# Two changes around a 1x1 convolution: seven block products in place of eight, and a residual added by accumulating transfers

## The chip, the cores and the metric

The kernel runs on one core of one Trainium2 chip. The core has five engines that each work through their own instructions in order: TensorE (matrix products; in the profile PE, its weight loads PEld), VectorE (DVE), ScalarE (ACT), GpSimd (POOL) and SyncE (SP), which here only issues transfers. POOL issues transfers too, on a queue of its own. Engines wait for each other and for transfers on semaphores. The metric is the device time of one execution in microseconds; given is the median of the runs. All data are 32-bit floats.

## The reference

Two layers on `x` of shape (4, 1024, 32, 32), that is 4 batches of N = 1024 tokens with C = 1024 channels. The first layer is attention with normed and rotated queries and keys, the second three convolutions with batch norms:

```python
# layer 0
q, k, v = split(x @ w_qkv.T + b_qkv)
q, k = rmsnorm(rope(q)), rmsnorm(rope(k))
ctx = softmax(q k^T / 8) v            # 16 heads of 64
out = rmsnorm(ctx @ w_proj.T) * norm_out_w
x1  = out + x                         # residual of layer 0
# layer 1
h = relu(bn(conv1x1(x1, w1) + b1))    # 1024 -> 256 channels
h = relu(bn(conv3x3(h, w2) + b2))
h = bn(conv1x1(h, w3) + b3)           # 256 -> 1024
y = relu(x1 + softplus(residual_scale) * h)
```

The batch norms take mean and variance over all four batches, so no value of the first 1x1 convolution can be used before the last batch's is there.

## The kernel before

All activations lie channels by tokens: a batch is eight rows of tiles [128 channels, 1024 tokens]. `half[0]` and `half[1]` are its two halves of 512 tokens, `NH` = 4 is half of the eight rows. The batches go one after the other through the projections of q, k and v, attention and the output projection `y`. The large projections (`project2`) are products of 2x2 blocks done with seven products in place of eight, in two levels; sums of blocks of the activations are made by VectorE, sums of weight blocks lie ready in DRAM. The first convolution (L850, `conv1`) is done plainly.

For batches 0 to 2, y after its norm is stored to DRAM (`x1d`), and `x` is added to it there by accumulating transfers that POOL issues during the next batch's attention (`add_residual`, L1034). Batch 3 has no attention after it. Its norm (`last_norm`, L826 to L841) works on y in place: `inverse_rms` makes the sum of squares over channels by a TensorE product with ones (`ss_y`, L666), then root, reciprocal and a round through DRAM back into `total` (tile `sqy`); then for each half and row VectorE multiplies y by it (L834) and adds `x` (L835) from the tile `xr`, which SP has loaded (L1095), and SP stores the result to `x1d` (L836). y of batch 3 stays in SBUF and is the input of its own convolution.

While that norm runs, TensorE does the first convolution of batches 1, 2 and 0, whose inputs are read back from `x1d` by `read_back` (tile `x` for batch 1, `back` for 2, `x_back` for 0), then that of batch 3. A call of `conv1` makes one of 2 x 2 output tiles of a batch (128 of 256 channels by 512 tokens) with eight matmuls into one bank of the pool `o2`; ScalarE takes it out with the bias, VectorE makes its statistics (L859) and SP stores it to `h1d` (L860). For batches 0 and 1 the tiles come back as `h1l` (L1128) and are filled into padded tiles for the 3x3 convolution (L1131, L1142, L1202). The weights `w_c_last` are four chunks of the ring `w` of eight; the weights `w3` of the last convolution (L1309) come into the same ring.

The order of the work is written out by hand: TensorE, POOL and, through this part, VectorE and ScalarE keep the order in which the program issues instructions. `after(n, step)` runs a step n products later, `waiting` holds steps that are taken one by one as there is room (`pace`), and `product_done` moves this clock. Only SP's transfers are ordered by a scheduler, at build time; on the chip SP then works through them strictly in that order, and each waits for what it needs. A transfer issued by SP also waits for the one eight places before it. Short-lived tiles of 128x512 come from the pool `tmp` with four buffers: a new one waits until the earliest free buffer's last reader, often a store, is done.

Of the kernel before, what the change touches and what calls it, by code (L numbers as in the profile page):

```python
# [12 lines left out]
AF = mybir.ActivationFunctionType  # L13
ALU = mybir.AluOpType
# [4 lines left out]
P = 128  # L19
B, C, H, W = 4, 1024, 32, 32  # L20
N = H * W
NT = C // P
HD = 64
NHP = C // (2 * HD)
CH = 512
NCH = N // CH
# [3 lines left out]
NPT = PL // P  # L30
# [31 lines left out]
NH = NT // 2  # L62
NG = NT // 2
QH = P // 4
SUMS = ("S2", "S1", "S3", "S4")
# [20 lines left out]
def program(ctx, tc, x, wblk, w2, w3, vecs, cos, sin, out, bad):  # L86


    nc = tc.nc
# [6 lines left out]
    x1d = dram.tile([NT, P, B * N], F32, name=f"x1d{u}")  # L96
    h1d = dram.tile([NPT, P, B * N], F32, name=f"h1d{u}")
# [13 lines left out]
    def col(name, i=0):  # L111
        return vec[:, COL[name] + i : COL[name] + i + 1]
# [30 lines left out]
    h1stats = const.tile([P, NPT, B * NCH, nc.vector.BN_STATS_DIM], F32, name="h1stats")  # L143
# [9 lines left out]
    with tc.tile_pool(name=f"st{u}", bufs=2) as st, ExitStack() as s:  # L153
# [25 lines left out]
        yt = {}  # L179
        half = [slice(c * CH, (c + 1) * CH) for c in range(NCH)]  # L180
# [17 lines left out]
        def bank(kind, name):  # L198
            pool, shape = psum[kind]
            return pool.tile(shape, F32, tag=kind, name=name)  # L200

        def temp(name):
            return tmp.tile([P, CH], F32, tag="tmp", name=name)

        def big_temp(name):
            return big.tile([P, N], F32, tag="big", name=name)

        def load_x(b, c, rows=range(NT)):
            for i in rows:
                nc.sync.dma_start(xs[b][:, i, half[c]], x[b, i * P : (i + 1) * P, half[c]])  # L210

        def chunk(name):
            return wring.tile([P, NH, P], F32, tag="w", name=name)
# [28 lines left out]
        TT = 0.21  # L242
        later, waiting = [], deque()
# [5 lines left out]
        def after(n, step):  # L249
            later.append((pace["at"] + n, step))  # L250

        def product_done(share=1.0):
            pace["at"] += share
            pace["room"] = min(pace["room"] + share, 1.2)
            due = [s for at, s in later if at <= pace["at"]]
            later[:] = [(at, s) for at, s in later if at > pace["at"]]
            for step in due:
                step()
            while waiting and pace["room"] > 0 and not pace["hold"]:
                next_waiting()  # L260

        def next_waiting():
            cost, step = waiting.popleft()
            spend(cost)
            step()
# [5 lines left out]
        def sums(ts, bs, i):  # L271

            at, low = slice(i, i + 2), slice(i + NH, i + NH + 2)
            b11, b12, b21, b22 = (bs[:, r, h] for r in (at, low) for h in half)
            t1, t2, t4 = (t[:, at, :] for t in ts)
            nc.vector.tensor_tensor(t1, b12, b11, ALU.subtract)
            nc.vector.tensor_tensor(t2, b22, t1, ALU.subtract)
            nc.vector.tensor_tensor(b12, b22, b12, ALU.subtract)
            nc.vector.tensor_tensor(t4, b21, t2, ALU.subtract)
# [377 lines left out]
        def inverse_rms(total, eps, scale, name, then):  # L657


            r = temp(f"rms_{name}")[:, :QT]  # L660
            row = inv_d[norms_done.pop(0)]

            def root():
                o = bank("o2" if name in ("q_0", "k_0") else "o1", f"ss_{name}")[:, :QT]
                for q in range(4):
                    nc.tensor.matmul(  # L666
                        o[q * QH : (q + 1) * QH, :], ones[:, :QH], total[:, q * QT : (q + 1) * QT],
                        start=True, stop=True,
                    )
                nc.scalar.activation(r, o, AF.Sqrt, bias=eps, scale=scale)  # L670
                after(0.5, invert)

            def invert():
                spend(3 * TT)
                nc.vector.reciprocal(r, r)
                nc.gpsimd.dma_start(row.rearrange("(q t) -> q t", q=4), r[::QH, :])
                nc.gpsimd.dma_start(total, row.partition_broadcast(P))
                after(2.5, then)

            after(4, root)  # L680
# [145 lines left out]

            inverse_rms(total, eps_rms, 1.0 / C, f"y_{b}", then)

        def last_norm(b, total, ys, xr):


            def norm(f, at):
                y = ys[:, f, at]
                nc.vector.scalar_tensor_tensor(y, y, col("ow", f), total[:, at], ALU.mult, ALU.mult)  # L834
                nc.vector.tensor_tensor(y, y, xr[:, f, at], ALU.add)  # L835
                nc.sync.dma_start(x1d[f, :, b * N + at.start : b * N + at.stop], y)  # L836

            def then():
                waiting.extend([(2 * TT, lambda f=f, at=at: norm(f, at)) for at in half for f in range(NT)])

            inverse_rms(total, eps_rms, 1.0 / C, f"y_{b}", then)  # L841

# [3 lines left out]
        def conv1(b, f, c, w, ys, then=None):  # L846
            o = bank("o2", f"c1_{b}_{c}_{f}")
            for i in range(NT):
                ih, ii = divmod(i, NH)
                nc.tensor.matmul(  # L850
                    o, w[f][ih][:, ii, :], ys[:, i, half[c]], start=(i == 0), stop=(i == NT - 1)
                )
                if i == NH - 1:
                    product_done()
            h = temp(f"h1_{b}_{c}_{f}")
            nc.scalar.activation(h, o, AF.Identity, bias=col("b1", f))

            def stats():
                nc.vector.bn_stats(h1stats[:, f, b * NCH + c, :], h)  # L859
                nc.sync.dma_start(h1d[f, :, b * N + c * CH : b * N + (c + 1) * CH], h)  # L860
                if then is not None:
                    then()

            after(1, stats)
            product_done()

        def norm_of(stats, g, be, name):
# [48 lines left out]
        def read_back(b, rows=range(NT)):  # L916
            for i in rows:
                nc.sync.dma_start(back[b][:, i, :], x1d[i, :, b * N : (b + 1) * N])

        def x_tile(b):  # L920
            return xp.tile([P, NT, N], F32, tag="x", name=f"x_{b}")

        def t_tiles(b):
            return [tp.tile([P, NH, CH], F32, tag=f"T{i}", name=f"t{i}_{b}") for i in range(3)]

        def v_room(name):
            return kv.tile([P, N // P, C], F32, tag="v", name=name)
# [47 lines left out]
        room = v_room("rq_0")  # L975
        for b in range(B):
# [67 lines left out]
            room = v_room(f"to_{b}")  # L1044
# [12 lines left out]
            if b + 1 < B:  # L1057
                xs[b + 1] = x_tile(b + 1)
                ts[b + 1] = t_tiles(b + 1)
                rows = (0, 1, 4, 5, 2, 3, 6, 7)  # L1060
                for j in range(NT):

                    def load(b=b, i=rows[j]):
                        for c in range(NCH):
                            load_x(b + 1, c, (i,))

                    after(3 + 1.5 * j, load)
                for i in range(0, NH, 2):

                    def queue(b=b, i=i):  # L1070
                        waiting.append((7 * TT, lambda: sums(ts[b + 1], xs[b + 1], i)))

                    after(3 + 1.5 * (2 * i + 3) + 2, queue)
            else:
                back = {1: x_tile(b + 1)}
                for i in range(NT):
                    after(8 + 1.5 * i, lambda i=i: read_back(1, (i,)))
            if b == 0:
                weight_parts([parts_of[WK][1]], 2, 0, 4, pieces_of(room[:, 3 * NT // 4 :, :]))
            yt[b] = kp.tile([P, NT, N], F32, tag="k", name=f"y_{b}")  # L1080
# [3 lines left out]
            ty = qk_proj(b, WP, q_all, tc_, None, yt[b], "y", None, two)  # L1084
            if b + 1 < B:
                o_norm(b, ty, yt[b])
            else:
                xr = v_room("xr")
                last_norm(b, ty, yt[b], xr)

        back[2] = kv.tile([P, NT, N], F32, tag="q", name="back")
        read_back(2)
        w = conv1_weights("last")
        for i in range(NT):
            nc.sync.dma_start(xr[:, i, :], x[B - 1, i * P : (i + 1) * P, :])  # L1095
        for b in (1, 2, 0):
            if b == 0:
                back[0] = x_tile("back")
                read_back(0)
            for c in range(NCH):  # L1100
                for f in range(NPT):
                    conv1(b, f, c, w, back[b])
        rest()
        if bad is not None:
            dt = temp("dens")
# [169 lines left out]
        for b in range(B):  # L1275
            steps = []
            if b + 1 < B:
                steps = transform(b + 1, 0) + transform(b + 1, 1)
# [5 lines left out]
            for f in range(NPT):  # L1284
                for h in range(2):
# [14 lines left out]
                    steps = steps[4:]  # L1300
# [9 lines left out]
            if b == 0 and bad is not None:  # L1310
                o = ps.tile([P, CH], F32, tag="mm", name="fit")
# [20 lines left out]
        for f in range(NT):  # L1332
            if f > 0 and f + 2 < NT:
                load_x1(f + 2)
            stats = st.tile([P, B * NCH, nc.vector.BN_STATS_DIM], F32, tag="s3", name=f"s3_{f}")
# [5 lines left out]
            for i, k in order:  # L1341
                b, c = divmod(i, NCH)
                nc.tensor.matmul(  # L1343
                    os[i], w3t[k][f // NH][:, f % NH, :], h2[b, k][:, half[c]],
                    start=(k == 0), stop=(k == NPT - 1),
# [3 lines left out]
                h = h3s[f % 2][:, b, half[c]]  # L1349
# [89 lines left out]
```

## Time and profile before

| | |
|---|---|
| median of 3 runs (2713.77 to 2715.1) | 2714.19 us |
| the profiled execution | 2712.96 us |
| its span, first to last instruction | 2711.0 us |
| TensorE busy | 2665.8 us, 98% of the span |
| VectorE busy | 2171.9 us, 80% |
| ScalarE / POOL busy | 1096.3 us, 40% / 448.5 us, 17% |
| mean granted TensorE clock | 0.996 |

The busy shares are means over stages. By stage around the change (from a table of windows, us from the span's start; busy is us of the stage's length):

| stage | length | PE | DVE | ACT | DMA share, GB/s |
|---|---|---|---|---|---|
| convolution of batch 1, 2359.78 to 2387.60 | 27.82 | 27.82 | 8.77 | 5.90 | 0.96, 362 |
| of batch 2, to 2415.10 | 27.50 | 27.50 | 24.12 | 2.75 | 0.90, 305 |
| of batch 0, to 2442.60 | 27.50 | 27.50 | 2.78 | 2.75 | 0.22, 80 |
| of batch 3, to 2470.10 | 27.50 | 27.50 | 12.59 | 5.42 | 0.48, 144 |

TensorE is busy without a break; VectorE is so only while batch 2 is done, when it norms y of batch 3; the DMA engines are full through the first two stages.

### The profile page before, as it was taken

Reading aid. Unit: us, or ns where it says so; the run is one execution under the profiler, and the core shown is the slowest. Engines: PE = TensorE matmul, PEld = TensorE weight load, DVE = VectorE, ACT = ScalarE, POOL = GpSimd, SP = SyncE. Lnnn points to the kernel's source line nnn. Section 1 sums busy time; section 2 is a strip of 40 time slices with the busy share of each in tenths; the row PEclk is TensorE's granted clock in tenths of the full one; section 3 lists DMA queues with packets and bytes.
Section 4 is the critical chain, followed back from the end, with each engine's and each line's share of the span. In section 5 each row is a group of like instructions: output and inputs, shape, how many; then the busy total and the mean of one; then the engine's idle time right before and its main releaser. Section 6 shows DMA issues by size and latency. Waiting matters only on the chain. (4 is left out here: it accounts for less than half of the span.)

```text
span 2711.0 us, 32574 instructions
## 1 busy us (share of the span) xinstructions
PE 2665.8 (98%) x11410; PEld 1658.3 (61%) x11410; DVE 2171.9 (80%) x2516; ACT 1096.3 (40%) x1520; POOL 448.5 (17%) x552
## 2 busy tenths in 40 slices
PE   9999999899999999999999999999999999999997
PEld 4448533387888433588886333888884335846843
DVE  5578899988798877888878877877888878646987
ACT  2222555323352555333343555233525653312266
POOL 2562223302111211100111211100111211000000
PEclk9999999999999999999999999999999999999999
DMA  7897645577677341456765420666783314662165
GB/s 277 315 308 223 182 151 170 181 242 257 220 206 212 67 93 32 143 152 221 188 184 153 84 58 17 212 200 177 188 233 82 71 40 130 195 242 86 63 226 210
DMA packets 245965, 453.54 MB, mean 167 GB/s; under 512 B 28385, under 2 KB 117265, under 8 KB 245793
## 3 DMA queue, kind: packets, MB, share of 16 engines
q1 hardware_dynamic: 203568, 310.72, 36.6%
q0 software_dynamic: 42224, 140.63, 19.7%
q8 instruction: 94, 1.54, 0.2%
q14 instruction: 79, 0.64, 0.1%
HBM read 316.71 MB, written 96.78 MB: 153 GB/s over the span
## 5 line engine op out<-in xcount | busy, mean ns | idle before, releaser
L768 DVE TENSOR_TENSOR den<-den,p 128x1024 f32<-128x1024 f32 x384 | 470.5, 1225 | 40.7 <-DVE den L766 0.5
L764 ACT ACTIVATE p<-sc 128x1024 f32<-128x1024 f32 x512 | 476.2, 1043 | 53.7 <-PE sc L757 53.6
L757 PE MATMUL sc<-q,k 64*128 64x512 f32 x2048 | 457.5, 596 | 0.0
L757 PEld LDWEIGHTS sc<-q,k 64*128 64x128 f32 x2048 | 190.2, 186 | 265.1 <-issue 121.4
L774 PE MATMUL cx<-p,to 128*64 128x512 f32 x1536 | 340.2, 595 | 0.0
L774 PEld LDWEIGHTS cx<-p,to 128*64 128x64 f32 x1536 | 106.0, 137 | 228.2 <-issue 228.2
L458 PE MATMUL p_y<-q,w_y 128*128 128x256 f32 x928 | 211.9, 382 | 5.6 <-DMA w_y<-in_wblk_dram 4.8
L738 POOL TENSOR_SCALAR q<-q,vec 128x512 f32<-128x512 f32 x64 | 122.7, 1923 | 564.2 <-DVE q L737 564.1
L453 PE MATMUL p_v<-w_v,x 128*128 128x256 f32 x928 | 209.7, 379 | 1.0 <-DVE x L424 1.0
L458 PEld LDWEIGHTS p_y<-q,w_y 128*128 128x128 f32 x928 | 176.9, 191 | 33.7 <-issue 9.7
L453 PEld LDWEIGHTS p_v<-w_v,x 128*128 128x128 f32 x928 | 176.2, 190 | 25.8 <-DVE x L424 1.4
L779 ACT COPY q<-cx 128x512 f32<-128x512 f32 x64 | 37.5, 587 | 357.0 <-PE cx L774 357.0
L458 PE MATMUL p_k<-to,w_k 128*128 128x256 f32 x672 | 153.1, 381 | 3.7 <-ACT to L547 3.7
L458 PE MATMUL p_q<-to,w_q 128*128 128x256 f32 x672 | 152.6, 380 | 0.4 <-ACT q L547 0.3
L458 PEld LDWEIGHTS p_k<-to,w_k 128*128 128x128 f32 x672 | 126.7, 190 | 25.0 <-ACT to L547 6.1
L458 PEld LDWEIGHTS p_q<-to,w_q 128*128 128x128 f32 x672 | 127.1, 190 | 20.3 <-ACT q L512 1.3
L766 DVE TENSOR_TENSOR den<-p 128x1024 f32<-128x1024 f32 x64 | 76.5, 1195 | 77.7 <-ACT p L764 77.7
L805 DVE RECIPROCAL rec<-dn 128x512 f32<-128x512 f32 x32 | 107.3, 3352 | 20.6 <-PE dn L799 20.6
L774 PE MATMUL cx<-p,rq 128*64 128x512 f32 x512 | 113.4, 595 | 0.0
L1343 PE MATMUL c<-h,w 128*128 128x512 f32 x256 | 110.3, 592 | 0.9 <-ACT h L1245 0.9
L700 POOL DMA_DIRECT2D k<-ks x64 | 55.4, 1012 | 278.4 <-ACT p L764 96.0
L458 PE MATMUL p_y<-to,w_y 128*128 128x256 f32 x384 | 90.1, 379 | 0.0
(438 smaller groups left out, 4182.2 us busy)
## 6 DMA issues: line engine op xcount, KB each, us to landing
w_v<-wd2f SPq DMA_DIRECT2D x112, 256.0 KB
w_y<-wd2f SPq DMA_DIRECT2D x112, 256.0 KB
w_q<-wd2f SPq DMA_DIRECT2D x84, 256.0 KB
w_k<-wd2f SPq DMA_DIRECT2D x84, 256.0 KB
x<-in_x_dram SPq DMA_DIRECT2D x64, 256.0 KB
q<-qs POOLq DMA_DIRECT2D x64, 256.0 KB, 5.6
k<-ks POOLq DMA_DIRECT2D x64, 256.0 KB, 4.5
inv<-rec SPq DMA_DIRECT2D x256, 64.0 KB
```

The costliest lines, as they stand in the source:

```text
L453: nc.tensor.matmul(o[:, q].rearrange("p (g f) -> p g f", g=2), r[:, i, q * P : (q + 1) * P], wt[:, :, i, :], skip_group_check=True, **at,)
L458: nc.tensor.matmul(o[:, q], wt[:, q, i, :], r[:, i, :], skip_group_check=True, **at)
L700: nc.gpsimd.dma_start(dst[i::2, f, :], other[1 - i :: 2, :], accum_op=ALU.add)
L738: nc.gpsimd.tensor_scalar(cx, cx, col("bv", hp), None, ALU.add)
L757: nc.tensor.matmul(sc[:, j], k_all[d, hp, t * P : (t + 1) * P], q_all[d, hp, at], start=True, stop=bad is not None,)
L764: nc.scalar.activation(p, sc, AF.Exp)
L766: nc.vector.tensor_tensor(d_, probs[0], p, ALU.add)
L768: nc.vector.tensor_tensor(d_, d_, p, ALU.add)
L774: nc.tensor.matmul(o[j * HD : (j + 1) * HD, :], v[:, t, h0 : h0 + HD], probs[t][:, j], start=(t == 0), stop=(t == N // P - 1),)
L779: nc.scalar.copy(q_all[:, hp, at], o)
L805: nc.vector.reciprocal(r, dn)
L1343: nc.tensor.matmul(os[i], w3t[k][f // NH][:, f % NH, :], h2[b, k][:, half[c]], start=(k == 0), stop=(k == NPT - 1),)
```

## The change

*Seven products.* For batches 1, 2 and 0 the 2x2 blocks of the weights (output channels by input rows; `A11` to `A22`) and of the input (`b11`, `b12` the upper rows' halves, `b21`, `b22` the lower ones') are combined into seven products of four matmuls each in place of eight: A11·b11, A12·b21, S2·T2, S1·T1, S4·b22, S3·(b22-b12), A22·(b21-T2). `conv1_sums` makes S1 to S4 from the weights on VectorE once, into the other four chunks of the ring. `t_sums` makes four differences per batch in eight VectorE operations of 128x1024; for batch 1 six of the eight are put into the last output projection, through `waiting`, with T1 in the unused last quarter of that batch's room. The products of a batch go into two banks that keep adding up (`o` of the pool `o1`, `o2`); ScalarE copies intermediate states out between products (`c11`, `c12`, `c22`, `c21`, and `c1p` from the second bank), and VectorE adds the parts. `conv1_rest` is a generator: after its first two products, A11 and A12 of the next batch are put in, then its last three (S4, S3, A22). Batch 0, the last, has none put in between. Batch 0 is read back into the tile `v` in place of the tile `x`.

*Last residual.* `last_norm` works on whole rows of 1024: L834 multiplies, then POOL issues a transfer that adds `x` from DRAM to y in SBUF, and SP's store to `x1d` follows it. `xr` and its loads are gone.

*What the build makes of SP's order.* From the weights of the first convolution on: `back` of batch 2 (8), store of c11 of batch 1, `back` of batch 0 (8), stores of c11 of batch 2, c12, c21 and c22 of batch 1, stores of y rows 1 to 5 (L836), store of c11 of batch 0, stores of y rows 6 to 8, stores of c12, c21 and c22 of batch 2, three w3 loads, store of c12 of batch 0, and then the first `h1l` load. The buffers of `tmp`: ScalarE's c1p of batch 0 takes over the buffer of c12 of batch 2, c21 of batch 2 that of c11 of batch 0.

```diff
@@ -826,17 +826,17 @@
 
             inverse_rms(total, eps_rms, 1.0 / C, f"y_{b}", then)
 
-        def last_norm(b, total, ys, xr):
-
-
-            def norm(f, at):
-                y = ys[:, f, at]
-                nc.vector.scalar_tensor_tensor(y, y, col("ow", f), total[:, at], ALU.mult, ALU.mult)
-                nc.vector.tensor_tensor(y, y, xr[:, f, at], ALU.add)
-                nc.sync.dma_start(x1d[f, :, b * N + at.start : b * N + at.stop], y)
+        def last_norm(b, total, ys):
+
+
+            def norm(f):
+                y = ys[:, f, :]
+                nc.vector.scalar_tensor_tensor(y, y, col("ow", f), total, ALU.mult, ALU.mult)
+                nc.gpsimd.dma_start(y, x[b, f * P : (f + 1) * P, :], accum_op=ALU.add)
+                nc.sync.dma_start(x1d[f, :, b * N : (b + 1) * N], y)
 
             def then():
-                waiting.extend([(2 * TT, lambda f=f, at=at: norm(f, at)) for at in half for f in range(NT)])
+                waiting.extend([(2 * TT, lambda f=f: norm(f)) for f in range(NT)])
 
             inverse_rms(total, eps_rms, 1.0 / C, f"y_{b}", then)
 
@@ -855,13 +855,99 @@
             h = temp(f"h1_{b}_{c}_{f}")
             nc.scalar.activation(h, o, AF.Identity, bias=col("b1", f))
 
-            def stats():
-                nc.vector.bn_stats(h1stats[:, f, b * NCH + c, :], h)
-                nc.sync.dma_start(h1d[f, :, b * N + c * CH : b * N + (c + 1) * CH], h)
+            def done():
+                keep_h1(b, f, c, h)
                 if then is not None:
                     then()
 
-            after(1, stats)
+            after(1, done)
+            product_done()
+
+        def keep_h1(b, f, c, h):
+            nc.vector.bn_stats(h1stats[:, f, b * NCH + c, :], h)
+            nc.sync.dma_start(h1d[f, :, b * N + c * CH : b * N + (c + 1) * CH], h)
+
+        def conv1_sums(w):
+
+            (a11, a12), (a21, a22) = w
+            s2, s1, s3, s4 = (chunk(f"c1_{o}") for o in SUMS)
+            nc.vector.tensor_tensor(s1, a21, a22, ALU.add)
+            nc.vector.tensor_tensor(s2, s1, a11, ALU.subtract)
+            nc.vector.tensor_tensor(s3, a11, a21, ALU.subtract)
+            nc.vector.tensor_tensor(s4, a12, s2, ALU.subtract)
+            return s2, s1, s3, s4
+
+        def t_sums(ys, t1, t2, i, steps=range(4)):
+
+            at, low = slice(i, i + 2), slice(i + NH, i + NH + 2)
+            b11, b12, b21, b22 = (ys[:, r, h] for r in (at, low) for h in half)
+            for out, p, q in [(t1, b12, b11), (t2, b22, t1), (b12, b22, b12), (b21, b21, t2)][steps[0] : steps[-1] + 1]:
+                nc.vector.tensor_tensor(out, p, q, ALU.subtract)
+
+        mine = {}
+
+        def four(o, wt, rows, first, last):
+            for i in range(NH):
+                nc.tensor.matmul(
+                    o, wt[:, i, :], rows(i), start=first and i == 0, stop=last and i == NH - 1,
+                    skip_group_check=True,
+                )
+
+        def conv1_first(b, ys, w):
+
+            o = mine[b] = bank("o1", f"c1_{b}")
+            four(o, w[0][0], lambda i: ys[:, i, half[0]], True, False)
+            h = temp(f"c11_{b}")
+            nc.scalar.copy(h, o)
+            product_done()
+            o2 = bank("o2", f"c1a_{b}")
+            four(o2, w[0][1], lambda i: ys[:, i + NH, half[0]], True, True)
+
+            def done():
+                nc.vector.scalar_tensor_tensor(h, o2, col("b1", 0), h, ALU.add, ALU.add)
+                keep_h1(b, 0, 0, h)
+
+            after(1, done)
+            product_done()
+
+        def conv1_rest(b, ys, w, ss, t1, t2):
+
+            o = mine[b]
+            four(o, ss[0], t2, False, False)
+            h12 = temp(f"c12_{b}")
+            nc.scalar.copy(h12, o)
+            product_done()
+            yield
+            o2 = bank("o2", f"c1s_{b}")
+            four(o2, ss[1], t1, True, False)
+            p5 = temp(f"c1p_{b}")
+            nc.scalar.activation(p5, o2, AF.Identity, bias=col("b1", 1))
+            product_done()
+            yield
+            four(o2, ss[3], lambda i: ys[:, i + NH, half[1]], False, True)
+
+            def done12():
+                nc.vector.scalar_tensor_tensor(h12, o2, col("b1", 0), h12, ALU.add, ALU.add)
+                keep_h1(b, 0, 1, h12)
+
+            after(1, done12)
+            product_done()
+            yield
+            four(o, ss[2], lambda i: ys[:, i, half[1]], False, False)
+            h22 = temp(f"c22_{b}")
+            nc.scalar.copy(h22, o)
+
+            def done22():
+                nc.vector.tensor_tensor(h22, h22, p5, ALU.add)
+                keep_h1(b, 1, 1, h22)
+
+            after(1, done22)
+            product_done()
+            yield
+            four(o, w[1][1], lambda i: ys[:, i + NH, half[0]], False, True)
+            h21 = temp(f"c21_{b}")
+            nc.scalar.activation(h21, o, AF.Identity, bias=col("b1", 1))
+            after(1, lambda: keep_h1(b, 1, 0, h21))
             product_done()
 
         def norm_of(stats, g, be, name):
@@ -1072,9 +1158,19 @@
 
                     after(3 + 1.5 * (2 * i + 3) + 2, queue)
             else:
+
                 back = {1: x_tile(b + 1)}
-                for i in range(NT):
-                    after(8 + 1.5 * i, lambda i=i: read_back(1, (i,)))
+                for j, i in enumerate((0, 1, 4, 5, 2, 3, 6, 7)):
+                    after(3 + 1.5 * j, lambda i=i: read_back(1, (i,)))
+                t1 = room[:, 3 * NT // 4 :, :].rearrange("p a (c t) -> p (a c) t", c=NCH)
+                t2 = {}
+
+                def first_sums(i):
+                    t2[i] = big_temp(f"t2_1_{i}").rearrange("p (a t) -> p a t", a=2)
+                    t_sums(back[1], t1[:, i : i + 2, :], t2[i], i, range(3))
+
+                for i in range(0, NH, 2):
+                    after(14 + 3 * i, lambda i=i: waiting.append((5 * TT, lambda: first_sums(i))))
             if b == 0:
                 weight_parts([parts_of[WK][1]], 2, 0, 4, pieces_of(room[:, 3 * NT // 4 :, :]))
             yt[b] = kp.tile([P, NT, N], F32, tag="k", name=f"y_{b}")
@@ -1085,21 +1181,34 @@
             if b + 1 < B:
                 o_norm(b, ty, yt[b])
             else:
-                xr = v_room("xr")
-                last_norm(b, ty, yt[b], xr)
+                last_norm(b, ty, yt[b])
 
         back[2] = kv.tile([P, NT, N], F32, tag="q", name="back")
         read_back(2)
         w = conv1_weights("last")
-        for i in range(NT):
-            nc.sync.dma_start(xr[:, i, :], x[B - 1, i * P : (i + 1) * P, :])
-        for b in (1, 2, 0):
-            if b == 0:
-                back[0] = x_tile("back")
-                read_back(0)
-            for c in range(NCH):
-                for f in range(NPT):
-                    conv1(b, f, c, w, back[b])
+        back[0] = v_room("back")
+        read_back(0)
+        conv1_first(1, back[1], w)
+        ss = conv1_sums(w)
+        for i in range(0, NH, 2):
+            t_sums(back[1], None, t2[i], i, range(3, 4))
+        room1, sums2 = t1, t2
+        rows1, rows2 = (lambda i: room1[:, i, :]), (lambda i: sums2[i // 2 * 2][:, i % 2, :])
+        for b, nxt in ((1, 2), (2, 0), (0, None)):
+            steps = conv1_rest(b, back[b], w, ss, rows1, rows2)
+            for _ in range(2):
+                next(steps)
+            if nxt is not None:
+                ys, new = back[nxt], {}
+                conv1_first(nxt, ys, w)
+                for i in range(0, NH, 2):
+                    new[i] = big_temp(f"t2_{nxt}_{i}").rearrange("p (a t) -> p a t", a=2)
+                    t_sums(ys, ys[:, i : i + 2, half[0]], new[i], i)
+            for _ in steps:
+                pass
+            if nxt is not None:
+                rows1 = lambda i, ys=ys: ys[:, i, half[0]]
+                rows2 = lambda i, new=new: new[i // 2 * 2][:, i % 2, :]
         rest()
         if bad is not None:
             dt = temp("dens")
```

## The prediction

> **What bounds the kernel now.** I read the chain of waits in order of time, then TensorE's timeline around the first convolution (L850), then the queues beside it. From the chain:
>
> ```profile
> 2275.11 84.83 PE p_y L458 x392
> 2359.94 13.73 PE c L850 x32
> 2374.24 96.34 PE c L850 x224
> 2473.62 1.26 ACT pad L1131
> ```
>
> From the last output projection to the end of the first convolution the chain is TensorE alone, so a microsecond saved or lost there moves the end. TensorE's timeline of the stage (start, length, operation, records):
>
> ```profile
> 2359.78 13.90 PE L850 MATMUL c<-x,w_c_last 128*128 128x512 f32 x32
> 2373.60 0.64 PE L666 MATMUL ss_y<-sqy,ones 128*32 128x256 f32 x8
> 2374.17 14.00 PE L850 MATMUL c<-x,w_c_last 128*128 128x512 f32 x32
> 2388.01 27.63 PE L850 MATMUL c<-back,w_c_last 128*128 128x512 f32 x64
> 2415.48 27.63 PE L850 MATMUL c<-x_back,w_c_last 128*128 128x512 f32 x64
> 2442.94 27.63 PE L850 MATMUL c<-y,w_c_last 128*128 128x512 f32 x64
> ```
>
> No gaps. A matmul is two records, a record costs (2415.48-2388.01)/64 = 0.429 us, a product of four matmuls 3.434 us. The mark to watch is 2442.94, where batch 3 starts; what follows hangs on it and shifts with it.
>
> **What the skill says.** (1) The Trainium skill, "DMA: Bandwidth & Descriptors", section "Queues, rings and completion order": a DMA engine takes turns, packet by packet, between the queues with work. So POOL's accumulating transfers and SP's stores will share the engines. In the trace both queues are busy together at 228 to 262 us (47.5% and 45.0%), which agrees. (2) The same page, "Anatomy of one DMA — SWDGE (gpsimd) path": some 2 us of a transfer are fixed, mostly the receipt of its last write. SP's lines show 4.3 us in all for a 256 KB store:
>
> ```profile
> 2443.86 0.32 SPq L860 DMA_DIRECT2D h1df<-h  x1
> 2444.27 0.38 SPq L1106 DMA_DIRECT2D dens<-densf  x1
> 2448.20 0.80 SPq L1128 DMA_DIRECT2D h1l<-h1df  x2
> ```
>
> The load at 2448.20 waits for the store issued at 2443.86. (3) "TensorE: Matmul & The Clock Gate", "Part 1: The HAM clock gate": after an idle window of about 3.4 us the clock halves until a busy one has passed. The trace agrees for waits of 4.4 and 4.8 us:
>
> ```profile
> 537.26 3.75 PE L458 MATMUL p_y<-q,w_y 128*128 128x256 f32 x8 [4.80 <-DMA w_y<-in_wblk_dram]
> 551.89 1.89 PE L458 MATMUL p_y<-to,w_y 128*128 128x256 f32 x8
> ```
>
> The same eight records take 3.75 instead of 1.89 us; the cost of such a wait is 1.6 to 2.5 us, I take 2.0.
>
> **The change part by part.** *Products.* Three batches go from 8 to 7 products: -3 x 3.434 = -10.3 us.
>
> *Sums in the projection.* Six VectorE operations of 128x1024 (1.16 to 1.23 us) in two lots of 3.65 us. Between 2322 and 2334 VectorE idles 4.9 us and at 2352.4 for 3.5 us; both lots fit to 0.2 us. Cost 0; without that cover, at most 0.2 us at the projection's end.
>
> *Weight sums.* In the built order VectorE does the bias addition of A12 first (it can start 0.2 us after TensorE is at 2366.65), then statistics, S1, S2. With 0.77, 0.61 and 0.72 us from start to start and 0.69 us for S2 (the pitches of L834 to L835, L859, L423 to L424), S2 is ready at 2369.63, TensorE goes on at 2369.75: +3.1 us. At most 2 more if the clock drops.
>
> *Turns of one bank.* A22 follows S3 in the same bank, with ScalarE's copy of the bank between, in all three batches; in the last batch (0) S4 also follows S1 directly. The second convolution shows this turn:
>
> ```profile
> 2544.46 1.03 PE L1202 MATMUL c2x<-V,t_w 128*128 128x256 f32 x4
> 2545.32 1.03 PE L1202 MATMUL c2y<-V,t_w 128*128 128x256 f32 x4
> 2545.52 0.59 ACT L1217 COPY c2x<-c2x 128x512 f32<-128x512 f32 x1 [5.54 <-PE c2x L1202]
> 2546.16 0.73 PEld L1202 LDWEIGHTS c2x<-V,t_w 128*128 128x128 f32 x4 [0.21 <-ACT c2x L1217]
> 2546.18 1.11 PE L1202 MATMUL c2x<-V,t_w 128*128 128x256 f32 x4
> ```
>
> From 2545.32, when c2x was finished, to 2546.18 are 0.86 us, there covered by c2y; here nothing covers them. With the slower first matmul 0.92: 4 x 0.92 = +3.7 us. So TensorE alone would give -10.3 + 3.1 + 3.7 = -3.5 us.
>
> *Residual by transfers: the queue behind it.* This decides. VectorE loses 16 additions, which were hidden. POOL gets eight accumulating 512 KB transfers, one per row of y after its L834 (1.28 us at 128x1024). SP's eight stores to x1d each wait for one of them, and SP works in order. In SP's new order the stores of rows 1 to 5 stand before the store of c11 of batch 0, and those of rows 6 to 8 before the store of c12 of batch 2. That last store frees the fourth `tmp` buffer, which ScalarE's `c1p_0` waits for, and TensorE's S4 of batch 0 waits for `c1p_0`. The old h1 stores had only short waits ahead of them.
>
> When does row 8 land? From 2369.75: S2, S1, the square sum's 0.57, A11 and A12 of batch 2 end at 2384.06; VectorE's addition and statistics, then eight sums (9.35 us), end at 2395.0; c12, c22 and their statistics at 2397.7; rows 1 to 8 of L834 are done from 2399.0 to 2408.7. The first transfer moves data from about 2400.4 (1.4 us after its issue, as at L700 and L1034). An accumulating transfer is slow:
>
> ```profile
> k<-ks POOLq DMA_DIRECT2D x2, 256.0 KB, 3.7
> DMA  0000000000000000949499498949971000000000
> ```
>
> Of this window of 8 us (bins of 0.2 us from 2084) the two transfers, 512 KB, fill 14: 2.8 us, 187 GB/s. The window 152 to 172 allows up to 216, the DRAM pairs of L1034 (two of 512 KB in 7 us, small transfers beside them) at least 150. Plain transfers of this stage:
>
> ```profile
> 2388.00:2416.00 28.00, 28.00 (x67) 12.44 (x66) 24.12 (x36) 3.07 (x5) 2.06 (x2) 1.00 0.91 305
> ```
>
> 305 GB/s at a share of 0.91 is 335, 1.56 us for 512 KB. Eight accumulates (22.4), seven stores between them (10.9) and c11 (0.8) make 34.1 us: row 8 lands at 2434.5. SP then issues its store and at 2434.8 that of c12, which lands 4.3 us later, 2439.1; `c1p_0` takes 0.69 and S4 starts at 2439.9.
>
> TensorE without this: S2 of batch 2 at 2395.3, S2 of batch 0 at 2420.2 (its sums are ready at 2417.8), S1 ends at 2427.1, S4 at 2428.0. So the wait is 12.8 instead of 0.9 us: +11.9, and the clock drop +2.0. Bounds: if the two queues overlapped perfectly, row 8 lands at 2423 to 2424, c12 at 2428, S4 at 2429 to 2430: +1 to +2, no drop. At 150 GB/s (28 us) and all stores added, row 8 lands at 2440: +17.5 and the drop. Nothing below zero: no store precedes its accumulate.
>
> *The rest.* The loads of xr (4 MB) go. Batch 0 is read back once t1 is free, at 2376.6, and lands by 2390, needed at 2402: hidden. The w3 loads move behind these stores and are first needed near 2592. The h1 loads come later but before the pad fill, which moves along with batch 3. Cost 0.
>
> *Sum.* -3.5 + 11.9 + 2.0 = +10.4 us. The profiled execution took 2712.96 (span 2711.0), 1.23 below the median 2714.19; 2712.96 + 10.4 = 2723.4, on the median 2724.6. I take 2724.
>
> **Rivals.** 0.2% is 5.4 us, about what can be told from no change.
>
> *A, the queue behind the accumulates (the forecast):* 2724, its own range 2719 to 2730. Chance 0.60. For it: the slow accumulate row and the built order. Against: the sharing is modelled, not seen.
>
> *B, on the other side, the transfers overlap:* if row 8 lands by about 2424, S4 starts some 1 us late and TensorE's own waits decide: -10.3 + 6.8 + 1 = -2.5 us, 2712. The point is row 8 at 2424; up to about 2422 the time would be 2710.7. For it: an accumulate leaves a third of the engines' time free in the row shown (mean of the filled bins about 7 tenths). Against: wherever both kinds run together the engines are full. Chance 0.20, with all in between that stays within 5.4 us.
>
> *C, the whole saving:* if weight sums and bank turns cost almost nothing and B holds: 2704 to 2708. The turn in the second convolution speaks against it. Chance 0.06.
>
> *D, the slow end:* the accumulates run at 150 GB/s, and both long waits of TensorE drop the clock: -3.5 + 17.5 + 4 = +18, 2732. Chance 0.14.
>
> **How the numbers follow.** Likeliest is A, 2724. The range must reach B's 2712 with some room and most of D: 2710 to 2732 leaves out C and half of D. Slower is A and D, 0.74; same is B, 0.20; faster is C, 0.06.
>
> **What would show it.** Right: 84 matmuls for batches 0 to 2; a gap of 3 us before the first S2 product, released by VectorE; gaps of 0.9 us before each A22; one gap of some 13 us before S4 of batch 0, released by ScalarE's c1p, itself late by the store of c12; SP waiting long for the accumulates; batch 3 starting near 2453. Wrong: row 8 landing before 2424, or c12's store not behind it; or a long wait at the S2 products of batches 2 and 0, which would mean VectorE was misjudged.

## The result, and the profile after

The changed kernel is slower: 2726.45 us, median of 5 runs (2720.67 to 2729.85), beside 2715.1 of the kernel before measured beside it (2713.77 to 2717.3). The ratio is 1.0044, its 95% interval 1.0032 to 1.0056. The profiled execution took 2720.67 us, span 2718.9, and is the fastest of the five. The forecast was 2724, range 2710 to 2732, slower with 0.74.

The chain of waits of the changed kernel, in order of time (start, length, what), names the cause; before, this stretch was TensorE alone:

```profile
2407.57 21.98 DMA y<-in_x_dram
...
2429.57 0.32 SPq L836
...
2429.98 4.91 DMA h1df<-c
...
2434.97 0.70 ACT c1p L924
...
2435.71 6.74 PE c1s L891 x8
```

Read it from the end. S4 of batch 0 (TensorE, 2435.71) waits for ScalarE's `c1p`, that for a store to `h1d` which lands after 4.91 us, that store for SP, which is busy with its store of a row of y (L836), and that for the last accumulating transfer, issued at 2407.57 and landed 21.98 us later. The data of the store to `h1d` were there long before. VectorE had finished them, c12 of batch 2, at 2419.81, 10.2 us before SP issued the store at 2429.98:

```profile
2419.06 0.75 DVE L930 SCALAR_TENSOR_TENSOR c<-c1s,vec,c 128x512 f32<-128x512 f32 x1
```

TensorE should have gone on meanwhile. Its timeline (start, length, operation, records, and in brackets the idle time before and who ended it) has four kinds of loss:

```profile
2358.45 3.60 PE L891 MATMUL c<-x,w_c_last 128*128 128x512 f32 x8
2361.88 3.60 PE L891 MATMUL c1a<-x,w_c_last 128*128 128x512 f32 x8
2368.53 3.67 PE L891 MATMUL c<-t,c_S 128*128 128x512 f32 x8 [3.06 <-DVE c_S L875]
...
2415.79 3.70 PE L891 MATMUL c<-back,w_c_last 128*128 128x512 f32 x8 [0.68 <-ACT c L938]
...
2422.76 3.60 PE L891 MATMUL c1s<-back,c_S 128*128 128x512 f32 x8
2435.71 6.74 PE L891 MATMUL c1s<-back,c_S 128*128 128x512 f32 x8 [9.36 <-ACT c1p L924]
...
2450.10 27.63 PE L850 MATMUL c<-y,w_c_last 128*128 128x512 f32 x64
```

A product without a wait starts 3.43 us after the one before. The first S2 starts 6.65 us after A12 (3.22 lost), each A22 4.27 or 4.28 after S3 (0.85 lost, three times), S4 of batch 0 12.95 after S1 (9.52 lost), and its eight records take 6.74 instead of 3.60 us, at about half the clock (3.1 lost; the granted clock is 0.53 from 2435 to 2442.3). The product that follows a short wait is itself some 0.1 us longer (3.67 or 3.70 instead of 3.60). From the first product of batch 1 to the start of batch 3 the stage lasts 2450.10 - 2358.45 = 91.65 us; before it was 2442.94 - 2359.78 = 83.16. So +8.5 us. What follows the start of batch 3 takes 268.8 us in place of 268.06. Below, "stage" means this length: it is free of what happens earlier, and earlier stages vary (last section).

### The profile page after: what moved, and what is told of

Its sections match the earlier page's. It is cut to its first block, busy times and chain, and to the rows that moved or that the text cites. A ratio compares the mean times of both kernels' runs of the same rounds, so it can differ in the third digit from the quotient of the medians.

```text
span 2718.9 us, 32557 instructions
## 1 busy us (share of the span) xinstructions
PE 2659.4 (98%) x11386; PEld 1653.8 (61%) x11386; DVE 2195.0 (81%) x2529; ACT 1097.7 (40%) x1523; POOL 457.8 (17%) x560
## 5 line engine op out<-in xcount | busy, mean ns | idle before, releaser
L700 POOL DMA_DIRECT2D k<-ks x64 | 56.1, 1032 | 280.0 <-ACT p L764 95.9
L453 PE MATMUL p_v<-w_v,t 128*128 128x256 f32 x384 | 90.1, 379 | 0.2 <-DMA w_v<-wdf 0.2
```

What stands on the lines that cost most here:

```text
L453: nc.tensor.matmul(o[:, q].rearrange("p (g f) -> p g f", g=2), r[:, i, q * P : (q + 1) * P], wt[:, :, i, :], skip_group_check=True, **at,)
L700: nc.gpsimd.dma_start(dst[i::2, f, :], other[1 - i :: 2, :], accum_op=ALU.add)
```

## The experiments

The kernels are compared by stage, and by time against the kernel before, whose medians were 2715.18 and 2715.69 us in two lots of runs on two chips.

| kernel | stage, us | time, us | ratio to before, 95% interval |
|---|---|---|---|
| before | 83.16 | 2715.18 / 2715.69 | |
| changed | 91.65 | 2726.45 | 1.0044 (1.0032 to 1.0056) |
| `after_again`, the same | 90.33 | 2724.69 | 1.0034 (1.0023 to 1.0046) |
| `e_pool_stores` | 80.70 | 2715.16 | 0.9996 (0.9988 to 1.0004) |
| `e_no_residual` | 81.55 | 2715.18 | 0.9999 (0.9991 to 1.0007) |
| `e_p5_big` | 88.04 | 2718.85 | 1.0009 (1.0001 to 1.0017) |
| `e_plain` | 81.86 | 2714.58 | 0.9994 (0.9986 to 1.0003) |
| `e_order` | 82.44 | 2714.01 | 0.9993 (0.9987 to 1.0) |
| `e_residual_alone` | 99.17 | 2733.03 | 1.0058 (1.0044 to 1.0072) |
| `e_both` | 72.96 | 2705.06 | 0.9958 (0.9945 to 0.9971) |

The theory: SP works in order; its stores of y wait for slow accumulating transfers, the convolution's own stores stand behind them, and through a buffer TensorE waits. The rivals: the load on the DMA engines makes the stores late in whatever queue; the seven products are too dear by themselves; VectorE is the bound.

### Stores of y out of SP's queue

```diff
                 nc.gpsimd.dma_start(y, x[b, f * P : (f + 1) * P, :], accum_op=ALU.add)
-                nc.sync.dma_start(x1d[f, :, b * N : (b + 1) * N], y)
+                if f == NT - 1:
+                    for g in range(NT):
+                        nc.gpsimd.dma_start(x1d[g, :, b * N : (b + 1) * N], ys[:, g, :])
```

> The changed kernel with the eight stores of y to x1d issued by POOL after its eight accumulating transfers, so that none of them stands in SP's queue ahead of the stores of the first convolution. Same products, same transfers. Theory (SP's queue behind the accumulates holds the store of c12 of batch 2, and with it c1p and S4 of batch 0): the gap of 12.95 us from S1 to S4 of batch 0 falls to the bank turn, about 4.3 us start to start, and S4's product takes 3.6 instead of 6.74 us; batch 3 starts some 11 to 12 us earlier than in the changed kernel, and the time is 2709 to 2714, about 3 us below the kernel before. Rival 1 (the load on the DMA engines itself makes the stores late, in whatever queue they stand): the gap stays at 8 us or more, time 2718 to 2727. Rival 2 (something later in the kernel, such as the stores of y landing late for the last stage, takes the gain back): gap gone at S4, but less than half of it arrives at the end.

TensorE's timeline at S1 and S4 of batch 0:

```profile
2428.47 3.60 PE L893 MATMUL c1s<-back,c_S 128*128 128x512 f32 x8
2433.50 3.70 PE L893 MATMUL c1s<-back,c_S 128*128 128x512 f32 x8 [1.43 <-ACT c1p L926]
```

The wait of 9.36 us is 1.43, the half clock is gone, and the stage is 10.95 us shorter with the same transfers and the same products. The edit also moves the stores of y behind all eight accumulates, but the link itself is seen: the store of c12 of batch 2, whose data are done at 2425.51, is issued at 2425.54 and no longer 10.2 us late. SP's queue it was. The whole gain reaches the end (268.05 us from the start of batch 3 on), so rival 2 falls. Rival 1 is true in a small part: the start of S4 is 5.03 us after S1 and not 4.3, because that store lands only about 2432.7, 7.2 us after its issue instead of 4.91, beside POOL's stores. The time, 2715.16, is 1.2 above the expected range; its sum started from a profile of before (2712.96) which is itself 2.2 us under the median of before in these runs. Against before the ratio does not differ from 1.

### The seven products without the accumulating transfers

```diff
-                nc.gpsimd.dma_start(y, x[b, f * P : (f + 1) * P, :], accum_op=ALU.add)
```

> The changed kernel without the eight accumulating transfers: x is not added to y of batch 3 in the last residual, that part is left out. SP's stores of y stay where they are and wait for VectorE only. Theory: this is the seven products alone, saving 10.3 us and paying 3.1 us for the weight sums and 3 to 4 bank turns of 0.9 us; S4 of batch 0 waits about 0.9 us; time 2709 to 2712.5. Rival (the seven products cost more than they save by themselves, through VectorE or the buffers): 2715 or more, with waits at the products of batches 2 and 0 that are not bank turns.

S4 waits 0.78 us, the four other waits are as in the changed kernel (3.06 and three of 0.68), and none stands at the S2 products of batches 2 and 0, where VectorE would show. That rules VectorE out. The stage is 81.55, 1.6 below before's; it holds one thing that the sum did not have: after the 3.06 us wait, S2's eight records take 5.18 us instead of 3.67, a half clock of 1.5 us. Without it the seven products alone save 3.1 us of their 10.3. The time, 2715.18, missed the expected range; a gain of 1.6 us in 2715 is within the interval.

### Another buffer for c1p of batch 0

```diff
-            p5 = temp(f"c1p_{b}")
+            p5 = big_temp(f"c1p_{b}")[:, half[0]] if b == 0 else temp(f"c1p_{b}")
```

> The changed kernel with one edit: c1p of batch 0 gets its buffer from another pool, so that ScalarE's copy from the S1 bank no longer waits for the store of c12 of batch 2. SP's order stays. Theory (the link from SP's queue to TensorE is that buffer): S4 of batch 0 loses this wait and starts a bank turn after S1; the next link of the same kind, c21 of batch 2 behind the store of c11 of batch 0 on ScalarE, stands ahead of c1p on the same engine, lands near 2429.9 in the changed kernel, and so still holds c1p until about 2431: gap of some 8 to 9.5 us start to start instead of 12.95, time 3 to 5 us below the changed kernel, 2719 to 2724. If that second link doesn't bind: gap 4.3 us and 2711 to 2714. Rival (not the buffer but the load on the engines): gap stays at 12 to 13 us, time as the changed kernel.

ScalarE's timeline shows the second link, `c21` of batch 2 (L949) in front of `c1p` (L924):

```profile
2438.76 0.69 ACT L949 ACTIVATE c<-c,vec 128x512 f32<-128x512 f32 x1 [13.90 <-DMA h1df<-c]
...
2439.81 0.70 ACT L924 ACTIVATE c1p<-c1s,vec 128x512 f32<-128x512 f32 x1
```

`c1p` no longer waits for a transfer, but ScalarE stood 13.90 us at `c21`, whose buffer the store of c11 of batch 0 holds. S4 starts 8.68 us after S1, as expected between 8 and 9.5; the wait falls from 9.36 to 5.08 us, the stage by 3.6 us. The time, 2718.85, is just below the expected range. So the link is the `tmp` buffers, and freeing one moves the wait to the next. That second wait is only in part the queue's: the data of c11 were done at 2418.22, SP issued its store between 2427.47 and 2428.88, and it landed about 2438.8, some 10 us later, with accumulates and row stores beside it. (S2 at half clock cost 1.7 us in this profile, 5.37 for 3.67.)

### Is it the accumulation that is slow?

```diff
-                nc.gpsimd.dma_start(y, x[b, f * P : (f + 1) * P, :], accum_op=ALU.add)
+                nc.gpsimd.dma_start(y, x[b, f * P : (f + 1) * P, :])
```

> The changed kernel with the accumulating transfers turned into plain loads of the same size, on the same queue, from the same place to the same place: x replaces y of batch 3, the sum of the two is left out. Theory (an accumulating transfer moves 190 to 210 GB/s, a plain one 335 to 400, and this slowness makes row 8 late): the last of the eight lands 6 to 10 us earlier than in the changed kernel, within some 14 us of its issue instead of 22.0; the wait ahead of S4 of batch 0 falls from 9.36 to 0.7 to 4 us; time 2713 to 2719. Rival (the latency of POOL's transfers and the turn between store and load on each row make it late, not the accumulation): landing and wait as in the changed kernel within 2 us, 2723 to 2728.

The queue, the order and the bytes of the writes are the same; only the addition is gone. Issue to landing of the eight transfers, first in the changed kernel, then here:

```profile
DMA to landing us min/median/max: 5.4/13.1/22.0
```

```profile
DMA to landing us min/median/max: 3.5/9.3/13.1
```

S4's wait falls to 0.90 us, and the stage is 81.86 us, a half clock of 1.7 us after S2 included. So the accumulation itself is the slow part, not POOL's issue nor the turn between load and store. Its rate by itself is seen in `e_pool_stores` from 2406 to 2414, with no store of y beside it; then, in the changed kernel from 2408 to 2428, accumulates and stores together; and in `e_plain` over the same 20 us, plain loads and stores together (each the DMA summary of its window):

```profile
DMA packets 413, 1.56 MB, mean 195 GB/s; under 512 B 36, under 2 KB 36, under 8 KB 412
```

```profile
DMA packets 1543, 5.49 MB, mean 274 GB/s; under 512 B 173, under 2 KB 173, under 8 KB 1542
```

```profile
DMA packets 2065, 7.32 MB, mean 366 GB/s; under 512 B 222, under 2 KB 222, under 8 KB 2064
```

The bytes are those written. 195 beside 366 is a factor of 1.9; the second figure is of loads and stores mixed. The Trainium skill, "Collectives: The Full Stack", section "The bandwidth ceiling: the fold count and why AG ≠ RS ≠ AR", measured a ratio of 1.93 between AllGather, which copies, and ReduceScatter, which adds in flight, and gives as reason that "the add needs two source reads". The page speaks of exchanges between cores; the ratio here is about the same, the reason is not shown by these runs.

### The order of products

```diff
-            four(o2, ss[3], lambda i: ys[:, i + NH, half[1]], False, True)
...
             four(o, ss[2], lambda i: ys[:, i, half[1]], False, False)
...
+            four(o2, ss[3], lambda i: ys[:, i + NH, half[1]], False, True)
...
-        conv1_first(1, back[1], w)
         ss = conv1_sums(w)
+        conv1_first(1, back[1], w)
```

(With S4 its step `done12` moves too.)

> The changed kernel with the order of products alone edited: weight sums issued to VectorE ahead of the first products of batch 1, S3 ahead of S4 in each batch. The stores of y stay in SP's queue. Theory: the 3.06 us wait at S2 of batch 1 and the turns of 0.7 us ahead of A22 go, some 5 us; in batch 0 ScalarE still stands behind the stores of c11 of batch 0 and c12 of batch 2, so one or two long waits remain at S3 or S4 of batch 0, 6 to 12 us together; the stage from the first product to batch 3 is 80 to 86 us instead of 91.65, time 2716 to 2722. Rival (the queue was late only because the products were late): all waits go as in e_both, stage 73 to 75 us, 2704 to 2708.

All small waits are gone. One long one stays, now at S3 (6.46 us, ended by ScalarE's copy of c12, which stands behind the same `c21`), with the half clock behind it:

```profile
2430.05 6.45 PE L891 MATMUL c<-back,c_S 128*128 128x512 f32 x8 [6.46 <-ACT c L918]
2436.33 3.60 PE L891 MATMUL c1s<-back,c_S 128*128 128x512 f32 x8
```

82.44 is in the expected 80 to 86; the time, 2714.01, is below the expected range. The stage is 9.2 us shorter than the changed kernel's, though the small waits, each with the slower product behind it, come to 3.3 + 3 x 0.95 = 6.1 us. The other 3.1 us are the long wait. S3 waits for ScalarE's `c21` and c12, which go on at 2428.83. `c1p` starts only at 2433.28, when the store of c12 of batch 2 has landed, but that is while S3 still runs (to 2436.3), so that S4 does not wait at all. The time lies 10.7 us under that of `after_again`, run beside it; what this is more than the stage's gain is not explained.

### The second half of the change alone

The kernel before, its eight products and old order kept, with the new `last_norm` and without `xr`:

```diff
...
-                nc.vector.tensor_tensor(y, y, xr[:, f, at], ALU.add)
-                nc.sync.dma_start(x1d[f, :, b * N + at.start : b * N + at.stop], y)
...
+                nc.gpsimd.dma_start(y, x[b, f * P : (f + 1) * P, :], accum_op=ALU.add)
+                nc.sync.dma_start(x1d[f, :, b * N : (b + 1) * N], y)
...
```

> The kernel before with the second half of the change alone: last norm on whole rows, x added by accumulating transfers, no xr; the first convolution keeps its eight products in the old order. The stores of y stand in SP's queue between the first and second half of batch 0's read-back. Theory (whatever stands behind those stores is late): TensorE waits in the first tile of batch 0 for rows of the read-back that are issued only after the last accumulate has landed, near 2425 to 2430, so the convolution of batch 0 starts or stops for 8 to 14 us and the time is 2722 to 2730. Rival 1 (the harm comes only from the link through the seven products' buffers): 2714 to 2717. Rival 2 (without the additions VectorE is done sooner and the read-back is early enough): a wait of 1 to 5 us, 2716 to 2720.

TensorE's timeline where batch 0 begins:

```profile
2420.05 3.60 PE L850 MATMUL c<-x_back,w_c_last 128*128 128x512 f32 x8
2436.83 26.85 PE L850 MATMUL c<-x_back,w_c_last 128*128 128x512 f32 x56 [13.18 <-DMA x_back<-x1df]
```

No seven products, no `tmp` link of theirs, and it is worse: 13.18 us of waiting, for four rows of `x_back` that SP issues only from 2430.85 on, behind the stores of y, and some 2.6 us of half clock (26.85 for 56 records, 24.2 at full clock). The wait is in the range, the time of 2733.03 is 3 above it, mostly by the clock. So whatever stands behind those stores in SP's queue is late, and rival 1 falls.

### The changed kernel again

> The changed kernel itself, profiled and timed again, because its first five runs lay 9 us apart while the stage around the change explains one length only. Theory (the stages before the change, which differ from run to run, and the clock drop after the 3.06 us wait make the spread): stage from the first product of batch 1 to batch 3 of 91.65 us, or 93.2 if S2's product falls to the half clock; start of that stage anywhere from 2358 to 2366; median 2722 to 2728. Rival (the transfers of this stage run in two ways, fast and slow): stage differs by more than 3 us from 91.65 at the same start.

The stage is 90.33, its start 2358.30, the wait at S4 9.52 us. The 1.3 us to the first profile are the half clock, with which S4 takes 5.25 us here and 6.74 there, less 0.2 us of longer wait. The transfers of the stage run alike in both: 22.0 and 21.8 us to the last landing.

### Both edits

The edits of `e_pool_stores` and `e_order` together:

> The changed kernel with two edits: the stores of y issued by POOL after the accumulating transfers, as in e_pool_stores, and a different order of products: the weight sums issued to VectorE ahead of the first products of batch 1, and S3 ahead of S4 in each batch, so that S4 covers the turn of the bank between S3 and A22, and S3 the turn between S1 and S4. Theory (the saving of 10.3 us was eaten by the queue, the turns of the bank and the wait for the weight sums): all three go, TensorE has no gap over 0.3 us from A11 of batch 1 to batch 3, the stage from there to batch 3's start is 73 to 75 us long instead of 91.65, time 2703 to 2707, below both kernels. Rival (VectorE, with statistics and sums for the next batch, becomes the bound once the turns are gone): gaps of 1 to 4 us ahead of the S2 products of batches 2 and 0, time 2708 to 2713.

The chain of waits at the end of the stage, TensorE alone again, each product 3.43 us:

```profile
2434.49 3.43 PE c L893 x8
2437.93 27.48 PE c L852 x64
```

TensorE waits for no semaphore in the stage; it is 72.96 us long, 10.2 less than before, which is the 10.3 us of the three products. 2705.06 us is 0.42% below before (interval 0.29% to 0.55%) and beats both kernels. The rival's waits at S2 of batches 2 and 0 do not appear.

## Why the prediction was right, and where its terms were off

The chain that it named is the chain of the profile, link by link: slow accumulates, SP in order behind them, the store of c12 of batch 2, its buffer, `c1p`, S4 of batch 0. Taking the queue away (`e_pool_stores`), one buffer (`e_p5_big`) or the slowness of the accumulation (`e_plain`) each shortened that wait by about what the theory says. By the terms of the sum:

| term | predicted, us | in the profile |
|---|---|---|
| three products fewer | -10.3 | -10.2, alone in `e_both` |
| weight sums before S2 | +3.1 | +3.3 |
| turns of a bank, three A22 | +2.8 (3 x 0.92) | +2.8 (3 x 0.95) |
| S4 of batch 0 | +12.8 | +9.5; +9.7 in the second profile |
| half clock after it | +2.0 | +3.1; +1.6 in the second profile |
| sum | +10.4 | +8.5; +7.2 in the second profile |

(The wait for the weight sums and the turns are given with the 0.1 us by which the product behind them is longer.)

Two terms were mis-sized. The first is the rate at which the two queues share the engines. The sum had 8.1 MB (eight accumulates, seven and a half stores) take 34.1 us, 238 GB/s; the window of the changed kernel shows 274, and row 8 landed at 2429.55, 71.1 us after the stage's start instead of 74.7. Its queues show why:

```profile
q0 software_dynamic: 760, 2.73, 68.4%
q1 hardware_dynamic: 782, 2.75, 36.7%
```

These are packets, MB and the share of the engines' time in the 20 us, first of POOL's queue, then of SP's. The shares add to 105%, so the model of one after the other held to within 5%. While they had the engines, the accumulates moved 200 GB/s, priced at 187, and the stores 375, priced at 335 from a stage of mixed transfers; in `e_no_residual` the same stores run at 376 GB/s (mean of 2404 to 2414). That 187 was so near is in part luck: it was read from the transfers of L700, which add from SBUF to SBUF, and nothing in the prediction showed that an accumulate from DRAM runs alike. Of the 3.6 us, some 0.6 came back: the store of c12 took 4.91 us to land, not 4.3. The second is the clock: 2.0 us was taken from waits of 4.4 and 4.8 us, and after 9.36 us it was 3.1, after 9.52 us 1.6.

In the first profile the two errors are opposite in sign, and the closeness of the time is in part luck too. The medians lie 11.35 us apart, the spans of the two profiled executions 7.9: +8.5 in the stage and +0.7 after it, less 1.3 because the stage began earlier. The median run of the changed kernel has a mean granted clock of 0.993, the profiled one 0.995; what the slower runs lost, and where, no profile shows.

One link was seen too simply. The prediction had ScalarE wait for one store; there are two, that of c11 of batch 0 first. In the changed kernel it ends earlier and costs nothing, so the number did not suffer, but a repair of the one buffer gives back only 4.3 us of 9.5 (`e_p5_big`). The page that the prediction names for a fixed cost of some 2 us speaks of transfers issued by GpSimd, while the store in question is SP's; the price in the sum, 4.3 us, was a measured one, so nothing hung on it.

The sums in the projection were costed at nothing: from its first matmul to the first product of batch 1 it takes 2358.45 - 2273.74 = 84.71 us, before 2359.78 - 2275.05 = 84.73. The w3 and h1 loads were too: `e_both` has them, its stage lacks no more than 0.1 us of the three products, and from the start of batch 3 on it takes 268.04 us, as before. In the changed kernel that part takes 0.7 us more, but its last 240 matmuls begin 149.73 us after the start of batch 3, before 149.72: what is lost is lost behind them, in the last norm and the last stores.

Rivals: row 8 landed well after the 2424 at which B decides. B would have been the outcome with plain transfers: `e_plain` gives 2714.58. C needed all waits gone and is what `e_both` does, 2705.06. D's rate of 150 GB/s did not occur; its half clock after S2's wait did, in three of the other profiles.

## What to carry to other kernels

A transfer queue that is worked in order passes a wait on to everything behind it: before a store is made to wait for a slow transfer, list what stands behind it in that queue, and who waits for those. Of the repairs tried, the largest gain in the stage from one edit came from putting the store on the queue of the transfer that it waits for (10.95 us; another buffer gave 3.6). And a product that goes on in a bank which is copied out between should have a product of another bank ahead of it: the new order of products and weight sums was worth 7.7 us (`e_pool_stores` to `e_both`; 3.3 of it are the weight sums) to 9.2 us (changed to `e_order`, where the long wait shrank too), almost as much as the three products.

## What the runs showed of the hardware that was not expected

- The length of the wait alone does not decide the half clock. Waits of up to 1.43 us in this stage were never followed by it, those of 5.08 us and more always. The same wait of 3.06 us before S2 left the eight records at 3.67 us in three profiles (both of the changed kernel, `e_pool_stores`) and slowed them to 5.18, 5.37 and 5.37 in three others. After 5.08 us of waiting eight records took 5.70, after 6.46 us 6.45, after 9.36 and 9.52 us 6.74 and 5.25. The Trainium skill, "TensorE: Matmul & The Clock Gate", "Part 1: The HAM clock gate", says that the window is free-running and the number of slow matmuls differs from run to run; this agrees. Its idle window of about 3.4 us is not a safe limit here: 3.06 us was enough in half of the cases. (The end of a matmul is modelled in the profile; from start to start the loss was 3.22 us.)
- A 256 KB store into full engines takes long to land: 4.9 us at the end of the changed kernel's row stores, some 7.2 in `e_pool_stores`, 9.7 for that of c11 of batch 0 in the changed kernel (issued by 2420.2, the next user of its buffer goes on at 2429.96).
- The stage began at 2358.30 to 2365.87 us in the profiles, though in the changed kernel and those made from it the program ahead of the stage is written alike. Runs of one kernel lie up to 11 us apart. The start differs by 7.6 us between these profiles, which are of different kernels; what moves it was not looked for. The granted clock moves too: the 12 runs of the changed kernel took 2724.9 to 2730.55 us where it was 0.992, and 2719.21 to 2724.49 us where it was 0.994 or 0.995. An effect of 2 us is seen in the stage's own length, not in the time of one run.
